# A two-layer perceiver on one core: the seams between its two cross attentions rewritten

## The chip, the cores and the metric

The kernel runs on one core of a Trainium2 chip, all in fp32. Its time is the device time of one launch in microseconds (us). A core has TensorE for matmuls (PE in the profile, with PEld for the loading of the stationary operand), VectorE (DVE), ScalarE (ACT), GpSimd (POOL) and SyncE (SP), which here issues almost all DMAs from one queue.

## The reference, cut to what matters

```python
# x (1, 128, 256), ctx_768 (1, 12544, 192); ln has no weights
x = x + L0_xattn(ln(x), ctx_768)   # 16 heads of 16, then an MLP 256-512-256 with relu
x = x + L0_attn(ln(x))             # causal self attention, 16 heads of 16
x = x + L0_ffn(ln(x))              # 8 experts 256-1024-256, gelu, two best per row
x = x + L1_xattn(ln(x), ctx_768)   # 16 heads of 64
x = x + L1_attn(ln(x))             # one head; probabilities < 0.01 go another way:
x = x + L1_ffn(ln(x))              # 8 experts: silu(x Wg) * (x Wu), then Wd, two best

def _L1_attn_ref(x, W):
    probs = softmax(x @ x.T / 16)
    vac = where(probs < 0.01, probs, 0).sum(-1, keepdims=True)
    sp = where(probs < 0.01, 0, probs); sp = sp / (sp.sum(-1, keepdims=True) + 1e-9)
    return sp @ x + 0.01 * (broadcast(vac) @ W.T)
```

The mixtures compute all eight experts for all 128 rows and weight each expert's output with a factor that is zero for the experts not chosen.

## The kernel before, in words

**Common parts.** The 128 rows of x lie on the 128 partitions. `layernorm` (L128 to L140) takes mean and variance on DVE, the standard deviation by a Sqrt activation on ACT (L135), and transposes the result on PE. ACT holds the tables of some functions at a time; a change of function brings an ACT_TABLE_LOAD, charged to the line that asks for it. A ring of 28 slots of SBUF, each 128 x 1024 fp32, is handed out in turn by `slot`; `slot_weight` (L60) takes a slot and has SP load a weight into it. `load_context` (L185) loads one block of the context with three DMAs on SP's queue: 128 of its 192 channels (lo, L193), and the other 64 (hi, L195) in two halves of columns, one above the other on the partitions. There are 13 blocks (NS) of up to 1024 keys. PSUM has two pools: two "wide" tiles of two banks each (`ps_s`, also under the name `ps_wide`) and four tiles of one bank (`ps_w`, also `ps_mm` and `ps_t`). A tile of a pool can be taken only when the earlier user of its memory has been read. Where `tc.manual_schedule()` stands, each engine's instructions run in the order of the text; elsewhere a scheduler sets the order.

**First cross attention** (0 to 460 us). Groups of keys go through scores on PE (L428, four row tiles of 32 partitions, 256 columns), the shift by a maximum (L506, POOL or DVE), exponentials (L517, ACT), the products with the values (L530, PE) and `gather` (L546), which puts each range's result into `accs`, ten ranges, five to an octet of heads. At the end (L675 to L702) both octets' ranges are brought to one maximum and added: one exponential for both (L682), one multiply over all of `accs` (L683), one reduce for each octet (L688), a reciprocal, a product and the bias. Then come the transposes of o, the MLP (L703 to L725) and the layernorm ln1.

**Fillers.** The keys of the second cross attention's first pass for all 13 context blocks depend on nothing computed here, so `first_keys` (L639) makes them as a generator: for each block k_s one step of hi products (L209) and two of lo products (L212), 39 steps in all; the copies out of PSUM (L655) are issued one step into the next block. `fill(n)` runs n steps wherever PE would have nothing to do, through the tail above, self attention and the first experts.

**Self attention** (L737 to L800). Queries and keys come out transposed, 128 channels (8 heads) to a chunk (a_pq, L745). `block_diagonal` (L158) multiplies each chunk of queries on DVE into 8 copies, each zero outside one head's 16 channels (qbd); a score product then uses all 128 rows (a_s, L766, eight for each chunk). The causal mask (L768) and the row maximum (L770) are DVE's, 16 exponentials (L773) ACT's. Three steps of filler follow, then p is transposed on PE, copied, multiplied with the values and a column of ones (av, L785, 17 columns a head), normalised, and projected (L798).

**First experts** (L803 to L877). `up` (L824) makes an expert's hidden rows, `between` (L832, L834) adds the bias and applies Gelu, `down` (L841) makes f_py. `up(e + 1)` precedes `down(e)`.

**Second cross attention** (L880 to L1175). 8 passes over the 13 blocks, two heads a pass: 104 periods t. One period t on PE: the products of p with v of period t - LAG (`attend`, L1043; LAG is NS + 1 = 14), the keys of the next block (L958 multiplies queries with keys; L209, L212 and L227, L234 make keys and values from the context). ACT copies the scores out of PSUM (`keep`, L975), DVE keeps a running maximum for each pass (L982). The maximum is known after the 13th block (`fold`, `pass_maximum`), is spread over the partitions by two one-row products and copied by ACT (`pass_spread`, L1017); then each tile of scores is shifted in place (`shifted`, L1024: POOL, in the last pass DVE), exponentials are taken (L1032), DVE reduces over the keys (L1066), and POOL adds the parts (L1071). In the last pass DVE adds whole tiles instead (L1062). `attended` (L1079, L1081) adds each block's product into an SBUF tile, and `pass_end` (L1089) adds the sums across partitions with products of ones, takes the reciprocal and scales. In the first pass (t below 13) the keys are those of the fillers, and further fillers and the queries of the other passes stand ahead of `keep`. The last 14 iterations, t from 104 on, have no scores of their own: they drain the last pass, each with a context load for the values. The weights of the output projection (`ywo`) are loaded behind the loop, then eight products of 128 x 256 and the bias (py, L1173) follow.

**Last stages** (L1178 to L1261), in the scheduler's order. l1a: ln4, the column sums of W (a1_pc, two products with ones, copied to SBUF), the similarity x x^T, its maximum and exponential (a_e), the split at 0.01, and the products with x. l1f: ln5, the router, then for each expert the loads of its three weights, gating and up products (L1249), Silu, the product on DVE (L1255) and f_py (L1258).

Of the kernel before, what the change touches and what calls it, by code (L numbers as in the profile page):

```python
# [33 lines left out]
def perceiver(ctx: ExitStack, tc: tile.TileContext, a: dict, out: bass.AP):  # L34
# [93 lines left out]

    def layernorm(x, name, bank=None):
# [5 lines left out]
        nc.scalar.activation(std, mv[:, 1:2], AF.Sqrt, bias=eps)  # L135
        rstd = small.tile([P, 1], F32, tag="rstd", name=name + "_rstd")
# [21 lines left out]
    def block_diagonal(pool, qT, chunk, qbd):  # L158

        nc.vector.tensor_tensor(  # L160
            qbd[:, 8 * chunk : 8 * chunk + 8, :],
            qT.unsqueeze(1).to_broadcast([P, 8, P]),
            headmask.unsqueeze(2).to_broadcast([P, 8, P]),
            ALU.mult,
        )

# [18 lines left out]
    def load_context(pool, name, s, bufs, queue=None):  # L185
# [4 lines left out]
        lo = pool.tile([P, SB], F32, tag="ctx_lo", name=name + "_lo", bufs=bufs)  # L190
        hi = pool.tile([P, SB // 2], F32, tag="ctx_hi", name=name + "_hi", bufs=bufs)
# [67 lines left out]
    def router(logits, name):  # L259
# [8 lines left out]
        nc.vector.reciprocal(rtot, tot)  # L268
        prob = small.tile([P, NE], F32, tag="r_p", name=name + "_p")
# [29 lines left out]
    with tc.tile_pool(name="l0w", bufs=1) as lw:  # L299
# [8 lines left out]
        with tc.tile_pool(name="l0x", bufs=1) as work, ExitStack() as ps0:  # L308
# [24 lines left out]
            NR = len(start_of)  # L333

            accs = work.tile([P, NR, 8, 17], F32, name="x0_accs")
            negmax = work.tile([P, NR, 8], F32, name="x0_negmax")
            ctxs = {}
# [212 lines left out]

            with tc.manual_schedule():
# [10 lines left out]
                for t in range(len(groups) + LAG + 1):  # L562
# [43 lines left out]
                    if t > LAG and last[t - LAG - 1]:  # L606
                        g = range_of[t - LAG - 1]
                        gather(g, oTs.pop(g))
            ps0.close()
            ctx.enter_context(psum_pool("ps1", 4))  # L610
            with tc.manual_schedule():
# [27 lines left out]
                def first_keys():  # L639
                    out = None  # L640
                    for s in range(NS):
                        if out:
                            out()
# [5 lines left out]
                        whole(0)  # L649
                        yield  # L650
                        whole(1)

                        def out(s=s, h=h, pk=pk):
                            for r in range(2):
                                nc.scalar.copy(firstk[s][:, r * h : (r + 1) * h], pk[r][:, :h])  # L655

                        yield
                    out()
# [3 lines left out]
                def fill(n):  # L662
# [7 lines left out]

                nr = NR // 2
                misc = slot("x0_misc")
                acc = misc[:, : 16 * 17].rearrange("p (j h d) -> p j h d", j=2, d=17)
                fall = misc[:, 272 : 272 + 8 * NR].rearrange("p (j b h) -> p j b h", j=2, h=8)
                om, o = misc[:, 352 : 352 + D], misc[:, 608 : 608 + D]  # L675
                allneg = small.tile([P, 2, 8], F32, tag="allneg", name="x0_allneg")
                by_octet = negmax.rearrange("p (j b) h -> p j b h", j=2)
                nc.vector.tensor_reduce(allneg, by_octet.rearrange("p j b h -> p j h b"), AX.X, ALU.min)
                nc.vector.tensor_tensor(
                    fall, allneg.unsqueeze(2).to_broadcast([P, 2, nr, 8]), by_octet, ALU.subtract  # L680
                )
                nc.scalar.activation(fall, fall, AF.Exp)  # L682
                nc.vector.tensor_tensor(  # L683
                    accs, accs, fall.rearrange("p j b h -> p (j b) h").unsqueeze(3).to_broadcast([P, NR, 8, 17]),
                    ALU.mult,
                )
                for j in range(2):
# [48 lines left out]
        with tc.tile_pool(name="l0a", bufs=1) as work, tc.manual_schedule():  # L736
# [26 lines left out]
            for g in range(2):  # L763
                st = ps_wide(f"a0_s{g}").rearrange("p a (b n) -> p (a b) n", n=P)
                for e in range(8):
                    nc.tensor.matmul(st[:, e, :], qbd[:, 8 * g + e, :], kT[:, g, :], start=True, stop=True)  # L766
# [111 lines left out]
    with tc.tile_pool(name="l1x", bufs=1) as work:  # L878
# [217 lines left out]
        with tc.manual_schedule():  # L1096
            for t in range(NP + LAG):
# [47 lines left out]
                if end:  # L1145
                    fold(periods[t][0])
# [166 lines left out]
```

## Time and profile before

| | us |
|---|---|
| median of 3 runs | 1596.02 (1594.2 to 1597.56) |
| profiled execution | 1592.66 |
| its span | 1590.9 |

The stages by time, each with the busy time of the engines in it, the mean granted clock of TensorE (1.00 is full speed) and the mean busy share of the DMA engines:

| stretch, us | what | PE | DVE | ACT | POOL | clock | DMA |
|---|---|---|---|---|---|---|---|
| 0 to 460.5 | first cross attention | 413.89 | 382.07 | 394.60 | 328.75 | 1.00 | 0.22 |
| to 481.1 | octets combined, MLP, ln1 | 19.63 | 9.32 | 5.09 | 0.12 | 0.92 | 1.01 |
| to 522.7 | self attention | 38.43 | 14.20 | 13.40 | 0 | 0.75 | 0.33 |
| to 584.7 | first experts | 61.44 | 17.92 | 13.16 | 0 | 1.00 | 0.61 |
| to 637.2 | second cross attention, first pass | 45.45 | 34.75 | 29.95 | 0 | 1.00 | 0.30 |
| to 1455.4 | its other passes | 810.58 | 628.08 | 489.48 | 519.77 | 1.00 | 0.28 |
| to 1524.6 | its drain and projection | 67.13 | 62.84 | 38.93 | 2.49 | 1.00 | 0.98 |
| to 1537.0 | similarity | 4.56 | 6.08 | 3.60 | 0 | 0.61 | 0.13 |
| to 1590.9 | last experts | 46.81 | 14.13 | 8.11 | 0 | 0.93 | 0.01 |

The page's first part gives the same for the whole span, with the number of instructions:

```profile
PE 1507.9 (95%) x17130; PEld 1156.8 (73%) x17130; DVE 1169.4 (74%) x1238; ACT 996.3 (63%) x1221; POOL 851.1 (54%) x559
```

A line of the timeline or of a table of groups names the start in us, the busy time, the engine, the line of the kernel, the operation, what it writes and reads by the program's names, the shapes, and how many instructions it puts together; in brackets stands the idle time before it and what ended that. Numbers in fences are us. A busy PE is not always a PE at its peak: at half the granted clock the same products take twice as long.

### The profile page before, as it was taken

The page shows a single profiled execution, that of the slowest core. Times are in us where ns is not written, and L with a number is a line of the kernel's source. Part 1 is how long each engine was busy: PE and PEld are TensorE (multiplying, and loading weights), DVE is VectorE, ACT ScalarE, POOL GpSimd, SP SyncE. Part 2 cuts the span into 40 slices and gives each one's busy share as a digit, 9 for nine tenths or more (in the row PEclk, how much of TensorE's full clock was granted, in tenths as well). Part 3 has the DMA queues.
Part 4 walks back from the last instruction along what each step waited for, and adds up shares of the span by engine and source line. Part 5 has one row for each costly group of instructions (what it writes and reads, how often), then busy time and mean ns, then how long its engine had stood idle before and what let it go on. Part 6 is the DMA issues. An engine that isn't in the chain of part 4 may idle for free.

```text
span 1590.9 us, 39751 instructions
## 1 busy us (share of the span) xinstructions
PE 1507.9 (95%) x17130; PEld 1156.8 (73%) x17130; DVE 1169.4 (74%) x1238; ACT 996.3 (63%) x1221; POOL 851.1 (54%) x559
## 2 busy tenths in 40 slices
PE   7999989999789998999999999999999999999978
PEld 4566666666545877877778787787787777777868
DVE  4798978999863327677777777777777777778952
ACT  5898979889853225665655665565665655655531
POOL 0588877888820000863863864864764764761000
PEclk9999999999997999999999999999999999999979
DMA  3211112111193661322222222232232222225930
GB/s 104 61 41 42 46 42 61 41 42 46 47 270 129 238 167 25 98 84 83 83 80 86 81 81 86 80 93 74 87 94 80 87 81 86 81 81 153 306 135 4
DMA packets 68737, 146.62 MB, mean 92 GB/s; under 512 B 8905, under 2 KB 27089, under 8 KB 68562
## 3 DMA queue, kind: packets, MB, share of 16 engines
q1 hardware_dynamic: 68258, 143.30, 30.0%
q8 instruction: 135, 2.21, 0.6%
q10 hardware_dynamic: 304, 0.79, 0.2%
q14 instruction: 40, 0.33, 0.1%
HBM read 143.92 MB, written 0.13 MB: 91 GB/s over the span
## 4 chain that ended last, share of the span: by engine, by line
PE 62%; DVE 6%; ACT 2%; POOL 1%; DMA 1%; issue 1%; SPq 0%; DVEq 0%; ACTq 0%
PE x_s L958 11%; PE x_v L234 10%; PE x_o L1043 10%; PE x_k L212 9%; PE x_v L227 5%; PE x_k L209 4%; PE f_h L1249 2%; PE f_h L824 2%; PE k L212 2%; PE f_py L841 2%; DVE x_part L1066 1%; POOL x_p L506 1%; PE k L209 1%; DVE x_folded L1005 1%; PE f_py L1258 1%
## 5 line engine op out<-in xcount | busy, mean ns | idle before, releaser
L1024 POOL TENSOR_TENSOR x_p<-x_p,x_spread 128x1024 f32<-128x1024 f32 (+1 forms) x175 | 402.6, 2324 | 165.1 <-ACT x_spread L1017 164.9
L506 POOL TENSOR_TENSOR x_p<-x_p,x_spread 128x512 f32<-128x512 f32 (+1 forms) x184 | 325.6, 1820 | 121.0 <-ACT x_spread L494 61.1
L1066 DVE TENSOR_REDUCE x_part<-x_p 128x256 f32<-128x1024 f32 (+1 forms) x175 | 329.4, 1923 | 1.6 <-ACT x_p L1032 1.6
L975 ACT COPY x_p<-x_s 128x1024 f32<-128x1024 f32 (+1 forms) x200 | 198.0, 996 | 177.7 <-DVE x_mx L982 97.9
L982 DVE TENSOR_TENSOR x_mx<-x_s,x_mx 128x1024 f32<-128x1024 f32 (+1 forms) x161 | 193.4, 1201 | 127.1 <-PE x_s L958 118.7
L1071 POOL TENSOR_TENSOR x_sums<-x_sums,x_part 128x256 f32<-128x256 f32 x161 | 118.7, 738 | 303.4 <-DVE x_part L1066 303.1
L441 ACT COPY x_p<-x_s 128x1024 f32<-128x1024 f32 x196 | 193.4, 1016 | 48.5 <-PE x_s L428 33.2
L234 PEld LDWEIGHTS x_v<-ywv_lo,x_ctx_lo 128*128 128x128 f32 x1568 | 189.3, 192 | 38.3 <-issue 36.8
L1032 ACT ACTIVATE x_p<-x_p 128x1024 f32<-128x1024 f32 (+1 forms) x200 | 197.8, 1037 | 1.4 <-DVE x_p L1024 1.3
L517 ACT ACTIVATE x_p<-x_p 128x1024 f32<-128x1024 f32 x196 | 196.3, 1062 | 0.2 <-DVE x_p L506 0.2
L1043 PE MATMUL x_o<-x_p,x_v 128*64 128x128 f32 x3136 | 193.6, 276 | 0.4
L234 PE MATMUL x_v<-ywv_lo,x_ctx_lo 128*128 128x128 f32 x1568 | 193.1, 276 | 0.0
L447 DVE TENSOR_TENSOR x_mx<-x_s,x_mx 128x1024 f32<-128x1024 f32 x140 | 168.2, 1221 | 32.1 <-PE x_s L428 17.2
L1043 PEld LDWEIGHTS x_o<-x_p,x_v 128*64 128x64 f32 x3136 | 169.6, 137 | 12.3 <-issue 1.5
L958 PE MATMUL x_s<-x_qT,x_kT 64*128 64x128 f32 x2744 | 177.7, 279 | 0.0
L212 PE MATMUL x_k<-x_ctx_lo,ywk_lo 128*128 128x512 f32 (+1 forms) x364 | 171.6, 594 | 0.0
L958 PEld LDWEIGHTS x_s<-x_qT,x_kT 64*128 64x128 f32 x2744 | 160.2, 188 | 15.6 <-issue 15.4
L943 ACT COPY x_v<-x_v 128x512 f32<-128x512 f32 (+1 forms) x208 | 116.2, 563 | 79.3 <-PE x_v L234 78.8
L227 PEld LDWEIGHTS x_v<-ywv_hi,x_ctx_hi 64*128 64x128 f32 x1568 | 106.8, 188 | 48.4 <-issue 25.1
L428 PE MATMUL x_s<-x_qz,x_kT 32*128 32x256 f32 x1568 | 117.6, 401 | 17.7 <-ACT x_p L441 16.6
L530 PE MATMUL x_o<-x_p,x_v 128*32 128x128 f32 x3136 | 111.7, 276 | 10.0 <-ACT x_p L517 8.5
L530 PEld LDWEIGHTS x_o<-x_p,x_v 128*32 128x32 f32 x3136 | 81.9, 109 | 53.9 <-ACT x_p L517 18.9
(257 smaller groups left out, 1761.1 us busy)
## 6 DMA issues: line engine op xcount, KB each, us to landing
x_ctx_lo<-in_ctxT_dram SPq DMA_DIRECT2D x119, 512.0 KB, 4.0
x_ctx_hi<-in_ctxT_dram SPq DMA_DIRECT2D x238, 128.0 KB, 3.8
f_w<-in_L_ffn_W_dram SPq DMA_DIRECT2D x32, 512.0 KB, 4.9
k_lo<-in_ctxT_dram SPq DMA_DIRECT2D x12, 512.0 KB, 10.0
f_gating<-n_kernel_gating_EDF_dram SPq DMA_DIRECT2D x8, 512.0 KB, 6.9
f_up<-L_ffn_kernel_up_EDF_dram SPq DMA_DIRECT2D x8, 512.0 KB, 7.5
f_wd<-ffn_kernel_down_EFD_dram SPq DMA_DIRECT2D x8, 512.0 KB, 7.3
k_hi<-in_ctxT_dram SPq DMA_DIRECT2D x24, 128.0 KB, 7.9
```

Of the source, the lines that this page charges most:

```text
L212: nc.tensor.matmul(ps[r][:, :h], wk[0][:, js], lo[:, r * h : (r + 1) * h], start=False, stop=True)
L234: nc.tensor.matmul(ps[r][:, kc * P : (kc + 1) * P], lo[:, r * h + kc * P : r * h + (kc + 1) * P], wv[0][:, js], start=False, stop=True, sk ...
L441: nc.scalar.copy(ps[t][k], st[k].rearrange("p a n -> p (a n)"))
L506: engine.tensor_tensor(v, v, by[:, banks].unsqueeze(2).to_broadcast([P, n, 2, 256]), ALU.add)
L517: nc.scalar.activation(ps[t][k], ps[t][k], AF.Exp)
L530: nc.tensor.matmul(os[b][32 * i : 32 * i + 32, u * P : (u + 1) * P], v[:, 2 * g + c, 17 * (2 * i + u) : 17 * (2 * i + u) + 32], p[i // 2][ ...
L958: nc.tensor.matmul(st[:, u, c * P : (c + 1) * P], kTs[t][rs, ks], qT[rs, j, :], start=True, stop=True)
L975: nc.scalar.copy(scores_kept(ps[t][i], sts[i].shape[2] // P), sts[i])
L1024: engine.tensor_tensor(v, v, spreads[j].unsqueeze(2).to_broadcast([P, 2, n, P]), ALU.add)
L1032: nc.scalar.activation(v, v, AF.Exp)
L1043: nc.tensor.matmul(o[us, 0:P], vs[t][:, c0 + c, us], p[:, n0 : n0 + P], start=(c0 + c == 0), stop=(c0 + c == total - 1), skip_group_check= ...
L1066: nc.vector.tensor_reduce(part, v, AX.X, ALU.add)
```

## The change

It touches every seam between the main loops; the main loops themselves keep their instructions. Part by part:

- **Tables.** `table` runs an activation on a one-column scratch tile, so that ACT changes its table there: to Sqrt ahead of each layernorm from ln1 to ln5, to Exp behind each standard deviation, to Gelu and Silu inside the routers' work.
- **Octets.** `octet` combines one octet. The first runs behind the last shift of the main loop, the second after it, and 3 steps of filler, not 6, stand ahead of the transposes of o; 2, not 3, ahead of ln1. `first_keys` copies each half out of PSUM right behind its products.
- **Self attention.** Instead of qbd, each chunk of queries is multiplied with two masks of parity (`qz`). The 16 score products use 32 rows each, in four row tiles with two heads to a tile, into both wide tiles; the heads come in another order, and the values and results are indexed by it. Filler: one step behind the scores, one behind each half of the exponentials, four then.
- **First experts.** Fewer fillers are left for them: in the built order the last two steps of k_8 stand behind the last f_py, not ahead of the first.
- **First pass.** Fillers and queries stand behind `keep`.
- **Last pass.** Both wide tiles are free for other use once its last scores are copied: one holds the running sums, the other the sum of all blocks' products (first half) and the projection (second half). DVE shifts the first tile of each period straight from PSUM, POOL the second one. `attended` does nothing in this pass. The projection weights are loaded at t = 105, seven of its eight products and the column sums of W follow at t = 107, and only one product is left at the end. Every third context from t = 106 on is loaded into slots of the ring. The last period's values are finished before the maximum is folded.
- **Last stages.** They are in the order of the text. The column sums are read from PSUM. All experts' weights are issued at once, behind all contexts, and gating and up of expert e + 1 precede the down products of e.

```diff
+    def table(func, name):
+        scratch = small.tile([P, 1], F32, tag="table", name=name)
+        nc.scalar.activation(scratch, eps, func)
...
         nc.scalar.activation(std, mv[:, 1:2], AF.Sqrt, bias=eps)
+        if bank is None:
+            table(AF.Exp, name + "_table")
...
+            def octet(j, out):
+                bs = slice(j * nr, (j + 1) * nr)
...
+                nc.scalar.activation(fall, fall, AF.Exp)
+                nc.vector.tensor_tensor(
+                    accs[:, bs], accs[:, bs], fall.unsqueeze(3).to_broadcast([P, nr, 8, 17]), ALU.mult
+                )
+                nc.vector.tensor_reduce(
+                    out.rearrange("p h d -> p (h d)"), accs[:, bs].rearrange("p b h d -> p (h d) b"),
+                    AX.X, ALU.add,
                 )
...
+                    if t == len(groups) + LAG - 3:
+                        octet(0, acc[0])
...
+                        for r in range(2):
+                            whole(r)
+                            nc.scalar.copy(firstk[s][:, r * h : (r + 1) * h], pk[r][:, :h])
+                            yield
...
+                octet(1, acc[1])
+                table(AF.Sqrt, "ln1_table0")
...
-                fill(6)
+                fill(3)
...
-                    block_diagonal(work, qT, j, qbd)
+                    for u in range(2):
+                        nc.vector.tensor_scalar(qz[:, j, u, :], qT, parity[:, u : u + 1], None, ALU.mult)
...
+            st = [ps_wide(f"a0_s{k}").rearrange("p a (b n) -> p a b n", n=P) for k in range(2)]
+            for g in range(2):
+                for u in range(2):
+                    for i in range(4):
+                        rs = slice(32 * i, 32 * i + 32)
+                        nc.tensor.matmul(
+                            st[i // 2][:, i % 2, 2 * g + u, :], qz[rs, g, u, :], kT[rs, g, :], start=True, stop=True
+                        )
...
+            fill(1)
+            for k in range(2):
...
+                if k:
+                    table(AF.Sqrt, "ln2_table0")
+                fill(1)
...
-            fill(3)
+            fill(4)
...
+            place = slot if t >= NP and (t - NP) % 3 == 2 else None
+            ctxs[t] = load_context(work, f"x1_ctx{t}", (t + 1) % NS, 2, place=place)
...
+                engine, by = nc.gpsimd, spreads[j]
+                if j == PASSES - 1 and (i == 0 or s == 0):
+                    engine, by = nc.vector, final["spread"][:, : 2 * P].rearrange("p (u q) -> p u q", q=P)
+                engine.tensor_tensor(v, v, by.unsqueeze(2).to_broadcast([P, 2, n, P]), ALU.add)
...
+            whole = j == PASSES - 1
+            o = final["both"][:, 0] if whole else ps_w(f"x1_o{t}")
...
+                if s == 0 and i == 0:
+                    nc.vector.tensor_copy(total, scores_kept(p, n))
                     return
...
+                if (s, i) == (NS - 2, len(tiles) - 1):
+                    sums[j] = work.tile([P, 2, KB], F32, tag="wide", name="x1_allsums")
+                nc.vector.tensor_tensor(sums.get(j, total), scores_kept(p, n), total, ALU.add)
...
+        def projected(j0, j1):
+            for j in range(j0, j1):
+                nc.tensor.matmul(
+                    final["both"][:, 1, :D], oT[:, j, :], ywo[j // 4][:, j % 4, :], start=(j == 0), stop=False
+                )
...
+                if t == NP + 1:
+                    context(t)
+                    ywo.extend(
+                        slot_weight(f"ywo{i}", a["L1_xattn_Wo"][512 * i : 512 * i + 512]) for i in range(2)
+                    )
+                if t == NP + 3:
...
+                    projected(0, PASSES - 1)
...
-                if t < NS:
-                    fill(2 if t < 4 else 1)
-                if t in (5, 7):
-                    queries(*((1, 5) if t == 5 else (5, 8)))
...
                     keep(t, sts, evicted if short else None)
+                if t < NS:
+                    fill(2 if t < 4 else 1)
...
+            nc.vector.tensor_tensor(oT[:, PASSES - 1, :], final["both"][:, 0, 0:P], os[PASSES - 1], ALU.mult)
+            projected(PASSES - 1, PASSES)
...
+    with tc.tile_pool(name="l1f", bufs=2) as work, tc.manual_schedule():
...
+        gu = [
+            [slot_weight(f"f1_{k}{e}", a[f"L1_ffn_kernel_{k}_EDF"][e]) for k in ("gating", "up")]
+            + [slot_weight(f"f1_wd{e}", a["L1_ffn_kernel_down_EFD"][e])]
+            for e in range(NE)
+        ]
...
         for e in range(NE):
...
+            if e + 1 < NE:
+                st = ps_wide(f"f1_h{e + 1}")
+                for i in range(2):
+                    up(e + 1, st, i)
+                following = fused(e + 1, st, gate(e + 1, st))
```

## What I predict before seeing the changed kernel run

> **What bounds the kernel now.** I read the rows by engine first, then the granted clock, then the chain of waits, and last the timeline of each stage that the change touches.
>
> ```profile
> PE   7999989999789998999999999999999999999978
> PEclk9999999999997999999999999999999999999979
> PE 62%; DVE 6%; ACT 2%; POOL 1%; DMA 1%; issue 1%; SPq 0%; DVEq 0%; ACTq 0%
> ```
>
> TensorE is full in almost every slice. The main loops of both cross attentions (0 to 460 us and 637 to 1455 us) hold the same instructions after the change, so the gain or loss lies in the seams between them: about 310 us, where PE is late for something or runs at half clock. These lines, from the timeline and from the table by stretches of 2 us (PE, PEld, DVE, ACT, POOL busy, then clock, DMA share, GB/s), show the seams:
>
> ```profile
> 461.39 1.57 DVE L683 TENSOR_TENSOR x_accs<-x_accs,x_misc 128x1360 f32<-128x1360 f32 x1
> 463.00 2.63 DVE L688 TENSOR_REDUCE x_misc<-x_accs 128x136 f32<-128x680 f32 x2
> 477.80 1.28 ACT L135 ACT_TABLE_LOAD   x1
> 479.10 0.29 ACT L135 ACTIVATE ln_std<-ln_mv,eps 128x1 f32<-128x1 f32 x1
> ...
> 485.58 3.84 PE L766 MATMUL a_s<-a_kT,a_qbd 128*128 128x128 f32 x32
> 492.97 2.03 PE L209 MATMUL k<-k_hi,k_wk_hi 64*128 64x512 f32 x2 [2.50 <-issue]
> ...
> 502.00:504.00 2.00, 2.00 (x16) 1.98 (x15) 0.00 (x0) 0.00 (x0) 0.00 (x0) 0.80 0.05 16
> 504.00:506.00 2.00, 2.00 (x11) 2.00 (x12) 0.78 (x2) 0.00 (x0) 0.00 (x0) 0.50 0.72 246
> ...
> 601.40 1.89 PEld L958 LDWEIGHTS x_s<-x_qT,k 64*128 64x128 f32 x32 [1.36 <-ACT x_p L975]
> 634.86 0.20 PEld L245 LDWEIGHTS x_mt<-ident,x_folded 128*128 128x128 f32 x2 [4.48 <-DVE x_kT L931]
> ...
> 1462.38 1.67 PE L227 MATMUL x_v<-ywv_hi,x_ctx_hi 64*128 64x128 f32 x16 [0.92 <-DMA x_ctx_hi<-in_ctxT_dram]
> 1520.24 3.72 PE L1173 MATMUL x_py<-ywo,x_oT 128*128 128x256 f32 x16
> 1585.67 1.99 PE L1258 MATMUL f_py<-f_wd,f_fuse 128*128 128x256 f32 x8 [1.41 <-DVE f_fuse L1255]
> ```
>
> The reader is to see serial DVE sums and a table load ahead of matmuls, a clock that halves in self attention (0.50), and PE waiting for a copy, a maximum, a transfer, and the last expert's product.
>
> **The sum, seam by seam.** Shifts are against the same event before; minus is earlier.
>
> *Combining the octets (L675 to L702).* One octet's multiply, reduce, fall and exponential move behind the last shift; DVE has none left after 456 and then idles 3.97 us for x_o. What remains behind the last gather is half the multiply (0.78 of 1.57) and one reduce (1.31 of 2.63), so o is ready 2.1 us earlier. Its exponential (0.25, L682) now stands ahead of ACT's last two: +0.25. Only 3 key steps, not 6, stand before PE's transposes of o: with k_0 alone PE reaches them at 466.9 and ends them at 467.4, not 469.85. Shift -2.45.
>
> *The square root's table loaded early.* ACT copies k until 477.79, loads 1.28, then takes std. The same copy still precedes std, so the load alone goes: -1.28, now -3.7. One k step (1.0 us) then lies between ln1's transposes and a_pq, half of it under the copy (+0.5), and the fourth a_pq waits for qT on DVE instead of ACT (+0.2): scores start at -3.0.
> The Trainium skill's ScalarE: Activation LUTs, section What ACT_TABLE_LOAD costs, asks 2.66 us a switch, 1.28 of it the load and 1.38 a drain. In this trace std starts 0.02 us behind the load and the load 0.01 behind the copy; no drain shows. Two loads leave the path alone (here and at ln4); the page's price would add 2.8 us to my gain. I take the row.
>
> *Self attention.* qbd (2 x 1.23 on DVE) becomes four small products, no longer late. The 16 score products in four row groups are not in this trace at N=128. Bounds: 3.84 us (no overlap) and 1.1 (32 passes at the 0.034 us of L530, four column groups). The nearest row group form, L428 at N=256, runs 16 passes in 1.08, 0.067 each; half the columns lies between, and I take 1.4. The page TensorEngine Tiling (Array Packing), Key Properties, warns that switching the tile mode drains TensorE; between L428 and the 64-row L209 behind it the trace shows 0.33 us of idle loads, so I put nothing more down.
> From the start S of the scores: DVE starts at S+1.5 (both banks fill together; before S+2.1) and needs 4.9 us for two masks and two maxima; a_v is copied by S+6.9; 16 exponentials of 0.30 end at S+8.9. PE meanwhile does k_2 to k_4, 7 steps of about 1.0, waiting 0.6 for the bank of a_v, to S+9.5. The transposes of p find all four banks held by k_3 and k_4, and ACT frees them only behind the exponentials and the new table load with its scratch (1.5): S+11.0. They start at S+12.9 before. The first a_v product starts at S+13.3, before S+16.4: -3.1, now **-6.1**.
> Behind it the order is as before. ln2's load also leaves, but four k steps (4.05 us of PE) gate its transposes at 522.72 anyway: 0.
> Clock: TensorE: Matmul & The Clock Gate, HAM oscillation, says no idle gap over about 3.4 us, no throttling. By that the 503.7 to 516.7 at half clock would not come back, worth another 6.5 us. But this trace throttles at 503.7 with no gap over 0.9 since 498.5, just behind sixteen 17-column products, and those stay. I take the row: it comes back.
>
> *First experts.* The Gelu table (1.28, L834) loads early, and k_8's second half (2.0 us of PE) moves from before the first f_py to behind the last: f_py starts at 532.5, not 534.1, -1.6. At the end those k products and two copies stand ahead of ln3's std: products to 584.5, copies to 585.2, std 585.2 against 585.38 with the shift included. Left: -0.2, now -6.3.
>
> *First pass of cross attention.* Copies of scores now precede those of keys on ACT. Before, scores 2 were copied at 600.33 behind a key copy that waited for PE; now at 597.9. DVE's 25 maxima (1.28 each) end at 630.1 instead of 632.3, and PE waits for them at 634.86: -2.15, now **-8.45**.
>
> *Last pass, drain (1447 to 1525).* DVE falls from 2 shifts, 2 sums and 1 add (5.2 us a period) to 1 shift and 2 sums (3.7); POOL takes a shift (2.36). PE stays at 1.09+1.98+1.90 = 4.97 a period and becomes the bound. Values ahead of the turn of the maxima, and shifts straight from PSUM: second attend at 1463.85, was 1466.23. Every third context lies in a slot of the ring, the first freed only when DVE has summed that tile (1463); its last part lands near 1467 (3.5 us), PE waits 1.3. Projection and column sums, 18 passes, 4.2 us, move in between. The later waits for contexts (2.4 us over seven periods; DMA share 0.98 here) go, because SP now sends the experts' weights behind all contexts. At the last attends: +0.9. Behind them 24 den passes (1.4), reciprocal and product (1.3), 2 projection passes and a row (1.0) instead of 8.4 us in all: -2.55. Together -1.65, now -10.1. The weights, 24 x 512 KB at the 360 GB/s seen here, take 35 us from about 1498 and are in before 1537.
>
> *Similarity and last experts.* a_pc (1.8 at half clock) leaves PE, and the exponential's table is there: a_e at 1529.45, was 1530.72; vs1 now in the chain: +0.18. -1.1. Gating and up of expert e+1 precede the products of e, so f_py 6 covers the last Silu and product: -1.41.
>
> Sum: -3.0 -3.1 -0.2 -2.15 -1.65 -1.1 -1.4 = **-12.6 us**. The profiled execution took 1592.66 (span 1590.9), so 1580.0; the median of the runs shown is 3.4 higher, 1596.02, giving **1583.4**.
>
> **Rivals.**
> 1. *The clock holds.* Denser k steps keep self attention warm: another -6.5, **1577**. For: the 2.50 us idle at 490.5 that precedes the first drop shrinks to 0.6. Against: the second drop had no such gap. 0.17.
> 2. *The drain gives nothing.* The 4.2 us of projection come in, and waits move from the experts' weights to slots that come free late: each of the 2.4 and the 2.55 above stays lost, -12.6+4.95, **1588**. For: DMA share 0.98, and SP serves in order. Against: later slots are free a period ahead. 0.16.
> 3. *Slower: half clock right through self attention.* If the short 32-row passes count as idle, the clock falls at the scores and stays at 0.5 until ln2. The work now at full clock there (485.6 to 490.5, 499.3 to 503.8, 516.7 to 522.7: 15.4 us) would take twice as long: -12.6+15.4, and the first experts' products double for some 3 us more: **1602**. It decides from 12.6 us of such work on. Against: L428's 32-row passes run at clock 1.00. 0.07.
> That the change does not do what it says is excluded: in the built order tables, fills, contexts and weights stand where the text puts them.
>
> **How the numbers follow.** Forecast 0.55 (1579 to 1588: score passes 1.1 to 3.84, slot wait 0 to 4), rivals 0.17, 0.16 and 0.07, and 0.05 for small losses adding up to no change. The range 1576 to 1591 leaves out the slower case and the tails. 0.2% is 3.2 us, about what a measurement can tell from no change: faster 0.88, same 0.04, slower 0.08.
>
> **What would show it.** a_s in 1.1 to 1.6 us and its DVE mask 1.5 behind its start; a_e near 1529.5 less the shift so far; DVE busy 3.7 of 5 us in the drain; one PE wait for x_ctx_hi early in it; no idle before the last f_py. Wrong would be: score passes at 0.12 us each, half clock outside 493 to 517, or contexts waited for in every third period.

## The result, and the profile after

The changed kernel takes 1575.58 us in the median of 4 runs (1573.13 to 1575.87), the kernel before 1595.55 in these comparisons: ratio 0.987, 95% interval [0.9853, 0.9888]. That is 20 us where I forecast 12.6, and the time lies just below my range. It is close to my first rival, "the clock holds", which I gave 0.17.

The page's rows of PE and of the granted clock by slices, and the chain of waits, of the changed kernel:

```profile
PE   7999989999879999999999999999999999999979
PEclk9999999999999999999999999999999999999979
PE 65%; DVE 7%; ACT 4%; issue 1%; DMA 1%; POOL 1%; DVEq 0%; ACTq 0%
```

The reader is to see that the 7 in the thirteenth slice of the clock, self attention, is gone. The timeline of the changed kernel has these lines for those that the prediction showed:

```profile
466.42 0.87 DVE L566 TENSOR_TENSOR x_accs<-x_accs,x_fall 128x680 f32<-128x680 f32 x1
467.32 1.36 DVE L569 TENSOR_REDUCE x_misc<-x_accs 128x136 f32<-128x680 f32 x1
479.78 0.30 ACT L140 ACTIVATE ln_std<-ln_mv,eps 128x1 f32<-128x1 f32 x1
480.09 1.28 ACT L132 ACT_TABLE_LOAD   x1
485.71 0.50 PE L770 MATMUL a_s<-a_kT,a_qz 32*128 32x128 f32 x6
486.23 1.05 PE L770 MATMUL a_s<-a_kT,a_qz 32*128 32x128 f32 x26
623.21 0.44 PE L246 MATMUL x_mt<-ident,x_folded 128*128 128x128 f32 x2 [2.68 <-DVE x_kT L950]
1454.30 1.51 PE L228 MATMUL x_v<-ywv_hi,x_ctx_hi 64*128 64x128 f32 x16 [0.34 <-DMA x_ctx_hi<-in_ctxT_dram]
1566.95 3.62 PE L1340 MATMUL f_py<-f_wd,f_fuse 128*128 128x256 f32 x16
```

Half the multiply and one reduce are left behind the last gather; the load comes behind ln1's standard deviation; the score passes run in some 1.57 us; PE waits 2.68, not 4.48, for the first maxima and 0.34 for one context; and the last two experts' products follow each other. The table by stretches of 2 us (PE, PEld, DVE, ACT, POOL busy, clock, DMA share, GB/s) shows what I had not expected:

```profile
500.00:502.00 2.00, 2.00 (x19) 1.85 (x19) 0.61 (x2) 0.00 (x0) 0.00 (x0) 1.00 0.72 246
502.00:504.00 2.00, 2.00 (x16) 1.52 (x13) 0.98 (x2) 0.58 (x1) 0.00 (x0) 1.00 0.04 16
504.00:506.00 2.00, 2.00 (x11) 1.20 (x13) 0.98 (x3) 0.24 (x1) 0.00 (x0) 1.00 0.00 0
```

These are the products with the values and what follows. Before, the same work ran into the half clock at 503.22 us and stayed there for 13.65 us, as the rows of 0.80 and 0.50 beside the prediction show.

Cutting both profiles at the same events gives the length of each stretch in us, beside what my sum put for it:

| from the event above to | before | after | change | predicted |
|---|---|---|---|---|
| last gather begins | 460.95 | 465.98 | +5.03 | 0 |
| o transposed | 8.91 | 5.97 | -2.94 | -2.45 |
| ln1 transposed | 10.68 | 9.27 | -1.41 | -1.25 |
| first score product | 5.05 | 4.49 | -0.56 | +0.7 |
| first product with the values | 16.45 | 13.50 | -2.95 | -3.1 |
| ln2 transposed | 21.15 | 14.54 | **-6.61** | **0** |
| turn of the first pass's maxima | 111.69 | 109.46 | -2.23 | -2.35 |
| turn of the last pass's maxima | 818.39 | 818.33 | -0.06 | 0 |
| ln4's standard deviation | 72.52 | 70.22 | -2.30 | -1.65 |
| ln5 transposed | 13.74 | 13.01 | -0.73 | -1.1 |
| last f_py | 48.17 | 45.80 | -2.37 | -1.4 |

Behind the first stretch the two profiles differ by 22.1 us. I take the first stretch for chance of the start. Of its 5.03 us, 4.20 are there already at score instruction 100 of the first cross attention (36.25 us before, 40.45 after): x came 2.15 us later in the profile after, and TensorE reached full clock at 21.10 us in place of 11.70. Two windows at half clock follow, at 236.14 and 437.53, where the profile of before has none. In the other profiles of this study without added products at the start, that of before_fill7 among them, score 100 came between 37.58 and 39.87 us and the last gather began between 463.2 and 466.1, so it was the profile of before that had a short start, as its 1592.66 against a median of 1595.55 also says. The medians, 20.0 us apart, lie between 17.1 and 22.1.

### The profile page after: what moved, and what is told of

Its sections match the earlier page's. It is cut to its first block, busy times and chain, and to the rows that moved or that the text cites. A ratio compares the mean times of both kernels' runs of the same rounds, so it can differ in the third digit from the quotient of the medians.

```text
span 1573.8 us, 39767 instructions
## 1 busy us (share of the span) xinstructions
PE 1498.2 (95%) x17138; PEld 1151.3 (73%) x17138; DVE 1153.5 (73%) x1219; ACT 997.9 (63%) x1233; POOL 873.4 (55%) x570
## 4 chain that ended last, share of the span: by engine, by line
PE 65%; DVE 7%; ACT 4%; issue 1%; DMA 1%; POOL 1%; DVEq 0%; ACTq 0%
PE x_s L977 11%; PE x_v L235 11%; PE x_k L213 10%; PE x_o L1069 10%; PE x_v L228 6%; PE x_k L210 4%; PE f_h L1302 2%; PE f_h L839 2%; PE f_py L856 2%; DVE x_part L1096 2%; PE x_both L1069 1%; ACT x_p L522 1%; PE k L213 1%; DVE x_folded L1024 1%; POOL x_p L511 1%
## 5 line engine op out<-in xcount | busy, mean ns | idle before, releaser
L1051 POOL TENSOR_TENSOR x_p<-x_p,x_spread 128x1024 f32<-128x1024 f32 (+1 forms) x186 | 427.5, 2325 | 151.4 <-ACT x_spread L1042 151.1
L1069 PE MATMUL x_o<-x_p,x_v 128*64 128x128 f32 x2744 | 169.6, 276 | 0.4
L1069 PEld LDWEIGHTS x_o<-x_p,x_v 128*64 128x64 f32 x2744 | 148.4, 137 | 11.0 <-issue 1.7
## 6 DMA issues: line engine op xcount, KB each, us to landing
f_gating<-n_kernel_gating_EDF_dram SPq DMA_DIRECT2D x8, 512.0 KB, 10.6
```

Of the source, the lines that this page charges most:

```text
L1051: engine.tensor_tensor(v, v, by.unsqueeze(2).to_broadcast([P, 2, n, P]), ALU.add)
L1069: nc.tensor.matmul(o[us, 0:P], vs[t][:, c0 + c, us], p[:, n0 : n0 + P], start=(c0 + c == 0 and (s == 0 or not whole)), stop=(c0 + c == tot ...
```

## Experiments

Each kernel ran in one of four groups, beside the kernel before on the same chip; the median of before differed from group to group (1596.75, 1591.71, 1592.99 and 1593.89 us), so kernels of different groups are set beside each other by their ratios to before, and single effects are read from the stretches of the table above, which repeat to some 0.1 us where the clock is the same.

### Why the clock held: again, few_fills, before_fill7

**again** and **after_b** are the changed kernel unaltered.

> The changed kernel a second time, unchanged. In its first profile self attention ran at full clock throughout: 14.5 us from the first product with the values to the end of ln2's transposes, where the kernel before took 21.1. Theory 'work': the seven dense steps of keys keep each 3.4 us window of the clock busy enough, so this profile shows 14 to 15 us again. Rival 'luck': where the windows lie decides, and this profile may show half clock and 18 to 21 us. Either way the median stays between 1573 and 1578.

Measured: 1577.04 us, ratio 0.9887 [0.9869, 0.9904]; the stretch from the first product with the values to ln2 took 14.54 us, as at first. In after_b it took 14.54 us too, and in the six variants that keep this stage's fillers (block_diag, drain_dve, three_seams, two_buffers twice, warm_all) again 14.54. The clock is no luck of one profile.

**few_fills**, three steps of keys ahead of the transposes of p:

```diff
-            fill(1)
             for k in range(2):
...
-                fill(1)
...
-            fill(4)
+            fill(3)
             load_pair(8)
```

> The changed kernel with three steps of keys ahead of the transposes of p, as before, in place of seven; the other four come later. Theory 'work': PE idles 3 to 4 us for p, the next windows run at half clock, the first a_v product to ln2's transposes takes 18 to 21 us in place of 14.5, and the kernel is 4 to 8 us slower than the changed one (1580 to 1584). Rival 'steps are only filler': the clock holds or falls as it did, and the time stays within 2 us of 1575.6.

Measured: 1583.74 us, ratio 0.9925 [0.9904, 0.9947]. Timeline of few_fills around the transposes:

```profile
489.41 1.12 PE L213 MATMUL k<-k_lo,k_wk_lo 128*128 128x512 f32 x2
492.76 0.63 PE L156 MATMUL a_pT_ps<-ident,a_p 128*128 128x128 f32 x4 [2.23 <-ACT a_p L783]
496.45 3.44 PE L797 MATMUL a_av<-a_v,a_pT 128*128 128x17 f32 x16
```

and its table by stretches of 2 us:

```profile
490.00:492.00 2.00, 0.54 (x2) 0.00 (x0) 1.97 (x2) 2.00 (x8) 0.00 (x0) 1.00 0.08 27
494.00:496.00 2.00, 1.74 (x6) 1.06 (x7) 0.81 (x2) 1.98 (x4) 0.00 (x0) 0.68 0.00 0
504.00:506.00 2.00, 2.00 (x11) 1.76 (x9) 0.00 (x0) 0.00 (x0) 0.00 (x0) 0.50 0.00 0
```

PE idles for p, the next window (a stretch of 3.41 us, explained with threshold below) is at half clock, and it stays there for 17.1 us: 22.99 us to ln2 in place of 14.54. The transposes start 4.0 us earlier, and still the kernel is slower.

**before_fill7**, one number in the kernel before:

```diff
-            fill(3)
+            fill(7)
             load_pair(8)
```

> The kernel before with one number changed: seven steps of keys ahead of the transposes of p in place of three. Theory 'work': no idle gap, clock at 1.00 behind the transposes, first a_v product to the end of ln2's transposes in 14 to 16 us in place of 21.1; with two steps fewer ahead of the first expert's down products the kernel gains 5 to 9 us (1587 to 1591). My blind reading (sixteen 17-column products throttle by themselves): the half clock stays behind the a_v products, the gain is 0 to 2 us.

Measured: 1589.87 us, ratio 0.9962 [0.9947, 0.9977]. Its table by stretches:

```profile
494.00:496.00 2.00, 0.66 (x2) 0.29 (x2) 1.24 (x2) 2.00 (x8) 0.00 (x0) 1.00 0.00 0
496.00:498.00 2.00, 2.00 (x4) 0.77 (x3) 0.00 (x0) 2.00 (x7) 0.00 (x0) 0.62 0.00 0
506.00:508.00 2.00, 2.00 (x19) 1.90 (x18) 0.30 (x1) 0.58 (x1) 0.00 (x0) 1.00 0.18 72
508.00:510.00 2.00, 2.00 (x15) 1.48 (x13) 1.29 (x2) 0.40 (x1) 0.00 (x0) 1.00 0.00 0
```

Here a gap is left (p comes later, since the scores take 3.84 us), and the clock falls once, for one window. The very same products with the values, from 505.8 on, then run at 1.00: 14.99 us to ln2, where the kernel before took 21.15. The sixteen 17-column products do not throttle by themselves. The kernel gains 6.9 us on the kernel before of its group.

### What the clock follows: probe, threshold

Both leave out the whole computation and run blocks of products of one kind. In probe these are products that stream 17 or 64 columns, 32-row tiles, 32-column tiles, transposes, and dense products (128 rows, 512 columns) with a wait for a copy after each one, two or three.

```diff
+    columns("c17", 220, 17)
+    dense("d1", 16)
+    columns("c64", 140, 64)
...
+    duty("u1", 12, 1)
```

> Leaves out the whole computation: only blocks of products of one kind each, 12 to 24 us long, with dense 128 x 512 products between them. If the clock follows the time in which TensorE is busy, the blocks of 17 columns, 64 columns, 32 rows, 32 columns of weights and transposes all stay at 1.00, and only the blocks with gaps (one, two or three 1 us products for each wait on a copy) fall. If it follows the share of the array that works (rows x columns x streamed columns), 17-column products, 32-row and 32-column products out of step fall to 0.50 within two windows of 3.4 us, and dense ones never do.

Measured, by the table of stretches of probe (PE, PEld, DVE, POOL busy, clock), for 17 columns, 64 columns, and one dense product for each wait:

```profile
35.00:112.00 77.00, 77.00 (x363) 77.00 (x362) 0.00 (x0) 0.00 (x0) 0.50 0.00 1
132.00:160.00 28.00, 28.00 (x253) 28.00 (x252) 0.00 (x0) 0.00 (x0) 1.00 0.01 1
285.00:303.00 18.00, 10.67 (x20) 2.68 (x18) 6.46 (x10) 0.00 (x0) 1.00 0.01 1
```

The first row is full without a gap and at half clock throughout; the last is idle 41% of the time and at full clock, with some 1,900 columns streamed in 3.41 us. So it is neither idle time nor busy time. The row and column tiles and the transposes stayed at 1.00 too, so my expectation that small tiles fall did not come true. But four tiles overlapped: a 256-column instruction on 32 rows took 0.054 us where a dense one of 512 columns takes some 0.43, so the array did about as much in a given time as in a dense block. Small tiles that do not overlap were not tried.

> Leaves out the whole computation: blocks of 220 products of 24, 32, 40, 44, 48, 52 and 56 columns, dense 128 x 512 products between. A window of 3.41 us that is full of dense products streams 4,079 columns; the self attention of the kernel before fell with 1,491 and stayed up with 1,539 and more. If the clock follows the columns streamed, blocks of 24, 32 and 40 columns (some 730, 980, 1,220 a window) fall to 0.50, 52 and 56 (1,590, 1,710) stay at 1.00, 44 and 48 lie near the edge. If it follows idle time, no block falls.

Measured, by the same table of threshold, for 48, 52 and 56 columns:

```profile
448.00:533.00 85.00, 85.00 (x414) 85.00 (x414) 0.00 (x0) 0.00 (x0) 0.52 0.00 1
553.00:598.00 45.00, 45.00 (x405) 45.00 (x405) 0.00 (x0) 0.00 (x0) 1.00 0.00 1
615.00:660.00 45.00, 45.00 (x405) 45.00 (x405) 0.00 (x0) 0.00 (x0) 1.00 0.01 1
```

24, 32, 40 and 44 columns fell as 48 did. The falls in the traces last a multiple of 3.41 us, unless the kernel ends in one, and lie on one grid of such windows through a whole run. In a window at full clock the 48-column products stream 1,468 columns over the array and the 52-column products 1,590, of 4,079 in a dense window: the edge lies between 36% and 39%. Once fallen, the 48-column block streams 768 a window and stays down for its remaining 84 us; dense products bring the clock back after one window in which they stream some 2,000.

The columns can be counted in all windows of the 14 profiles of whole kernels (some 6,350), weighted by the share of the array's rows and columns in use (512 columns on 64 of 128 rows count 256). That gives the same edge: the clock fell after no window with more than some 1,600, and under twenty windows below 1,460 were followed by full clock, nearly all in the first cross attention. Without the weights no edge shows: the clock then fell after windows with up to some 6,000 columns and held after some 2,800 windows with fewer. A single count is good to some 70 columns, because products lie across the ends of windows and some records are missing. In self attention of the kernel before, the window ahead of the second fall had some 1,500 (1,491 to 1,561 by two ways of counting); in the changed kernel the lowest had some 1,700, in its repetition 1,650. These cases alone would not settle the edge; threshold does.

Where the grid lies is chance, so I slid a window of 3.41 us along self attention of the changed kernel in steps of 0.01 us. By this estimate some window comes under 1,500 columns for 9% of the places where the grid can lie, and under 1,600 for 15%; the lowest has some 1,350. None of the nine profiles at 14.54 us had its grid there. The seven steps make a fall unlikely, not impossible, and in no_tables, with the same seven steps but the transposes of p 1.14 us sooner, one window of self attention did fall.

### What the parts are worth: block_diag, no_tables, three_seams

**block_diag** puts the block diagonal back:

```diff
-                        nc.tensor.matmul(
-                            st[i // 2][:, i % 2, 2 * g + u, :], qz[rs, g, u, :], kT[rs, g, :], start=True, stop=True
-                        )
+                    nc.tensor.matmul(
+                        st[k][:, n // 4, n % 4, :], qbd[:, head, :], kT[:, head // 8, :], start=True, stop=True
+                    )
```

> The changed kernel with the block diagonal of queries in place of the row tiles; everything else stays. As my prediction had it, the row tiles matter: score products take 3.84 us in place of 1.57, start up to 1 us later behind the two 1.23 us products on DVE, and the first product with the values moves by 2.5 to 3.5 us, the time with it (1578 to 1581). Rival: the seven steps of keys and the chain of p cover it, 0 to 1 us.

Measured: 1576.41 us, ratio 0.991 [0.9889, 0.9931]. The scores take 3.84 us and start 0.97 later, but the transposes of p then follow 8.20 us behind them in place of 9.44: net 2.0 us from ln1 to the first product with the values. The clock holds here too (14.54 to ln2). The row tiles are worth 2.0 us, less than the 2.5 to 3.5 that I expected; the seven dense steps, not the tiles, hold the clock.

**no_tables** makes `table` do nothing.

> The changed kernel without the early table loads; each load returns to the instruction that needs it. By the row of the trace (1.28 us a load and no drain): 1.28 us each at ln1, ln4, the exponential of the similarity and ln5, 0 at ln2, ln3 and in the experts, where PE has other work: 4 to 5.5 us slower than the changed kernel. By the price of 2.66 us a switch: 9 to 11 us.

Measured: 1579.68 us, ratio 0.9931 [0.9912, 0.9951], nearer to the row's 1.28 us a load than to the page's 2.66 (a loss of 9 to 11 us): from the last gather to the last f_py it took 5.9 us longer than in the profile of the changed kernel, part of it clock. By stretches: ln1 1.42 longer, the similarity with ln5 0.97. At the square roots of ln4 and ln5 nothing, since ACT loads a table as soon as it is free, while the input is still on its way. Its timeline at the end of the drain:

```profile
1508.06 0.64 ACT L1056 ACTIVATE x_p<-x_p 128x512 f32<-128x512 f32 x1
1508.71 1.28 ACT L139 ACT_TABLE_LOAD   x1
1515.02 0.30 ACT L139 ACTIVATE ln_std<-ln_mv,eps 128x1 f32<-128x1 f32 x1 [5.03 <-DVE ln_mv L137]
```

One early load costs: without the one for ln2 the transposes of p come 1.14 us sooner behind the scores, since it stands ahead of the copies that free their banks. The rest of the loss goes with the clock: one window fell at 499.4 and two from 577.9 on that do not fall in the changed kernel.

**three_seams** puts back three places:

```diff
-                    if t == len(groups) + LAG - 3:
-                        octet(0, acc[0])
...
+                octet(0, acc[0])
                 octet(1, acc[1])
...
+                if t < NS:
+                    fill(2 if t < 4 else 1)
...
                 if o is not None:
                     added(before, 0)
...
-                for i in range(2):
-                    up(e + 1, st, i)
+                up(e + 1, st, 0)
...
+            if e + 1 < NE:
+                up(e + 1, st, 1)
```

> The changed kernel with three seams put back that lie far apart: both octets combined behind the loop, fillers and queries of the first pass ahead of the copies of scores, and in the last experts only gating of expert e + 1 ahead of the down products of e. By my sums: last gather to the transposes of o 2.1 us longer, ln3 to the turn of the first maxima 2.15 longer, last experts 1.4 longer: 5.6 us in all. Rival: hidden at one or more of the three places, then under 0.5 us there.

Measured: 1585.64 us, ratio 0.9954 [0.9939, 0.9968]. The three expectations came out at 0, 8.2 and 2.0 us. From the last gather to the transposes of o it took 4.60 us, as in the repetition: the first octet's multiply still ran ahead of the last gather, so this place was not undone and its worth is not shown by this run. The first pass lost 8.2, far more than the 2.15 that I forecast against the kernel before. There the copies of keys were issued a step late; here they stand right ahead of the scores' copies on ACT and wait for PE (4.85 us for the one at 580.38), and PE then waits for the scores' copies. Its timeline:

```profile
579.22 1.98 PE L213 MATMUL k<-k_lo,k_wk_lo 128*128 128x512 f32 x4
582.80 2.08 PE L976 MATMUL x_s<-x_qT,k 64*128 64x128 f32 x32 [1.59 <-ACT x_p L993]
588.38 2.08 PE L976 MATMUL x_s<-x_qT,k 64*128 64x128 f32 x32 [1.59 <-ACT x_p L993]
```

So the two edits (copies at once, fillers behind `keep`) belong together; no run has fillers ahead of `keep` with late copies in the changed kernel, so this is a reading of the timeline.

### The drain: drain_dve, two_buffers

**drain_dve** has all last shifts on DVE:

```diff
-                if j == PASSES - 1 and (i == 0 or s == 0):
+                if j == PASSES - 1:
```

> The changed kernel with all shifts of the last pass on DVE, straight from PSUM, none on POOL. By my prediction DVE becomes the bound of the drain: 4 operations of about 1.25 us are 5.0 us a period against 4.97 of PE, so 0 to 3 us slower, all of it between the turn of the last maxima and ln4. Rival: PE stays the bound and nothing moves (under 0.5 us).

Measured: 1577.27 us, ratio 0.9924 [0.9898, 0.995]; the drain took 72.06 us in place of 70.22, 1.84 more. POOL's share is worth that much. PE's period stays 4.97 once it runs; the loss lies ahead of that, in one period of 7.52 us where the profile of the changed kernel has 5.68.

**two_buffers** loads no context of the drain into the ring (`place = None`).

> The changed kernel with all contexts of the drain in the two buffers, none in the ring. If the contexts' landing is what the ring's slots save, PE waits for x_ctx_hi or lo again and the stretch from the turn of the last maxima to ln4 grows from 70.2 by 1 to 3 us; if the weights of the experts standing behind all contexts was enough, it grows by under 0.5 us.

Measured: a median of 1581.08 us, but runs from 1574.14 to 1581.45, and the profile among the fastest (drain 70.61). So it was run again beside the unchanged kernel:

> The kernel without ring slots for the drain's contexts again, beside the changed one on the same chip. If the slots save what the single runs suggest (1581 against 1576), its profile or its median is 3 to 6 us slower, with waits of PE for x_ctx in the drain. If the first profile was right, both lie within 1.5 us.

> The changed kernel a third time, unchanged, beside the one without ring slots: 1574 to 1578; full clock from the first product with the values to ln2's transposes (14.5 us) for a third time if the density of the steps decides it.

Measured: 1575.53 (1570.06 to 1579.26), ratio 0.9883 [0.9855, 0.991], against 1575.66 (1574.6 to 1578.82), ratio 0.9893 [0.9869, 0.9916]; drains of 71.96 and 69.68 us. In the profiles the slots are worth 0.4 to 2.3 us (two_buffers_b has two waits for a context, 1.5 us together); in the times nothing that these runs can tell. What made three runs of the first group 5 us slower stays open.

### A faster version: warm_all, best

**warm_all** adds products that nobody reads where PE waits:

```diff
+                for i in range(14):
+                    nc.tensor.matmul(early[:, 1, 0:P], ones, ones, start=True, stop=True)
                 tiled()
...
+    def warm(name, n):
+        t = ps_w(name)
+        for i in range(n):
+            nc.tensor.matmul(t, ones, awT.rearrange("p c n -> p (c n)"), start=True, stop=True)
```

> The changed kernel plus products that nobody reads where PE waits: 14 at the start while the first weights come, 4 ahead of the turn of the first pass's maxima, and 2, 4 and 3 in the similarity stage. If the clock follows the work in each 3.4 us window, the half clock there goes: about 3 us at the start (score product 100 at 35 to 37 us), about 3 from ln4 to the second expert's products, 0 to 1.6 behind the first pass; median 1567 to 1571. Rival: the added products delay the real ones by what they save, and the time stays within 2 us of 1576.

Measured: 1573.37 us, ratio 0.9891 [0.987, 0.9913], no better than the changed kernel. Start and end gained (score instruction 100 came at 34.30 us; in the profiles without added products it lay between 36.25 and 40.45), but the four products ahead of the first maxima waited for a bank of PSUM and then ran in front of the real ones: that stretch grew by 3.54 us.

**best** leaves those out, spreads the others better (1, 2, 3 and 3 at the end), and drops the early load for ln2.

> The changed kernel with the added products kept where they helped (14 at the start; 1, 2, 3 and 3 from the last reciprocal to ln5) and without the early square root ahead of ln2, which stood between the exponentials and the copies that free PSUM for the transposes of p. Clock theory: no half clock between ln4 and the second expert's products (last reciprocal to second expert's products 2.5 to 4 us shorter), 1 to 3 us at the start, and p's transposes 1.1 us earlier: 5 to 7 us faster than the changed kernel, ratio to before 0.982 to 0.985. Rival: the added products stand in the way, ratio 0.986 or more.

Measured: 1565.62 us (1563.42 to 1566.01), ratio 0.983 [0.9811, 0.9848], below the whole interval of the changed kernel. The table by stretches of 5 us of best, in the similarity stage:

```profile
1501.00:1506.00 5.00, 4.22 (x15) 1.96 (x15) 2.04 (x7) 1.78 (x3) 0.00 (x0) 1.00 1.07 371
1506.00:1511.00 5.00, 3.23 (x10) 1.28 (x10) 3.14 (x13) 1.86 (x3) 0.00 (x0) 1.00 1.06 374
```

and of the changed kernel:

```profile
1514.00:1519.00 5.00, 1.22 (x4) 0.93 (x4) 2.78 (x12) 1.85 (x3) 0.00 (x0) 0.50 1.07 373
1519.00:1524.00 5.00, 1.67 (x3) 0.69 (x3) 2.52 (x9) 0.96 (x2) 0.00 (x0) 0.50 1.06 375
```

The half clock of 17.1 us is gone: from ln4's standard deviation to the first f_py of the last experts it took 19.47 us in place of 23.39. Without the early load for ln2 the first product with the values comes 1.5 us earlier. The last gather begins 7.3 us earlier than in the profile of after; how much of that the products at the start give, and how much is chance of the start, these runs do not separate.

## Why the prediction was right and wrong

**The step that failed** is in self attention: "By that the 503.7 to 516.7 at half clock would not come back, worth another 6.5 us. But this trace throttles at 503.7 with no gap over 0.9 since 498.5, just behind sixteen 17-column products, and those stay. I take the row: it comes back." It did not come back in any profile of the changed kernel, and that stretch gained 6.61 us. It is true that no long gap preceded the fall, but I made a cause of what merely stood beside it. The clock record puts the fall at 503.22, not 503.7: 1.2 us into the 2.53 us of the first of these products, and the window that ended there held transposes and one key step as well. The 17-column products are light work, and in before_fill7 they run at full clock. They pull a window under the edge only if the rest of it is light too: before, it came to some 1,500 weighted columns; with the work as the changed kernel orders it, to some 1,650 or more. I had put the denser steps down only as a filler for a wait, 0.6 us of idle time in place of 2.50, and they decided over the clock of the next 20 us. My first rival said that denser key steps keep the clock. It came true, though I argued for it with idle time, and idle time is not what the clock followed.

Neither was the rule that I set against the row the right one. The Trainium skill, TensorE: Matmul & The Clock Gate, section HAM oscillation, speaks of idle gaps over about 3.4 us; here the clock fell behind a gap of 2.23 us in few_fills and behind none at all in threshold. The same page's Part 1 says that the clock is set in free-running windows of 3,413 ns; the traces agree (falls of 3.41 us and its multiples on one grid), and from that, a count for each window would have been the view to make.

**Mis-sized terms.** I put +0.7 us between ln1 and the scores, and it was -0.56. block_diag splits this: with qbd the stretch is 5.46 us, so all else there, the key step above all, costs 0.41 (0.5 forecast for the step), and the four small products in place of qbd gain 0.97, a gain that I had put at nothing. The drain gave 2.30 for 1.65: the slot wait that I had at 1.3 us was 0.34. The last experts gave 2.37 for 1.41: besides the wait ahead of the last f_py, the step from one expert to the next fell from 5.41 or 5.42 to 5.30 us (seven steps give 0.8). In the timelines the gating products lie in one piece now, where the down products split them before; that this is the reason no run tested. The early tables ahead of ln4 did nothing, as no_tables shows.

**What held.** The octets with three steps of filler fewer (-2.94 for -2.45, with one window at half clock in both profiles; -4.3 in the repetition, which has none there), the table ahead of ln1 (no_tables loses 1.42 there), the first product with the values 2.95 earlier (3.1), the first experts and the first pass together (2.23 for 2.35), the main passes without change, DVE at 3.8 us and PE at 4.97 us a period in the drain. The price of a table load was the row's. Apart from the clock and the start, the terms add to 15.5 us where I had 12.6; with these alone the time would have come out within my range. The third rival, half clock right through, expected the clock to turn on how light the work is, as it does, but with the wrong sign: 32-row tiles do not count as idle when four overlap.

## What to carry to other kernels

Where a clock record shows half clock, lay the 3.41 us grid over the trace and add up, for each window, the columns streamed weighted by the share of the array that they use: under an edge between 36% and 39% of a dense window (as measured here) the next one runs at half speed, however busy PE looks, and light work at half speed keeps itself there. Filler belongs where a window is about to fall under that edge, and there a product that nobody reads can pay (best), as long as it does not stand in front of a real one (warm_all lost 3.54 us so). A table load that is moved early must not stand ahead of copies that free PSUM (1.14 us in this kernel).

## What the runs showed of the hardware

- The edge of the clock: 48 columns a product (1,468 of 4,079 a window) fell to 0.50, 52 columns (1,590) stayed at 1.00, both without a gap (threshold).
- Products with 32 rows or 32 columns, four overlapping, and dense transposes kept the clock at 1.00, for 34.8, 20.0 and 10.6 us (probe).
- Light work holds itself down: 48 columns a product stream 1,468 a window at full clock, 768 once the clock has halved, and stayed at 0.50 for the remaining 84 us (threshold).
- ACT starts a table load before the input of the activation that asks for it is there: at 1508.71 us in no_tables, 6.3 us ahead of that activation.
